# A four-layer graph network on one core: three engines and GpSimd put into the order of the source, and layer 0's products dealt out over the edge products

## The chip, the cores and the metric

The kernel runs on one core of a Trainium2 chip. The metric is device time in microseconds (us), the median of several runs. Engines are named as the profile names them: PE is TensorE's matmuls, PEld its weight loads, DVE is VectorE, ACT is ScalarE, POOL is GpSimd and SP is SyncE. In this kernel SP issues nearly all DMAs and computes nothing.

## The reference, cut to what matters

A graph of 3125 nodes with 128 features each and 103125 edges (src, dst, weight) goes through four layers. After each, the layer's output is added to its input and normalized over the features.

```python
# layer 0: weighted sum over the edges
out = relu(segment_sum(edge_weight[:, None] * (x @ weight)[src], dst) + b)
# layer 1: attention with 4 heads, softmax over the edges that reach a node
e = leaky_relu(a_s[src] + a_d[dst], 0.2); p = exp(e - segment_max(e)[dst])
out = segment_sum(h[src] * (p / segment_sum(p)[dst]), dst) + bias + x @ skip_W + skip_b   # then a layer norm of its own
# layer 2: dot-product attention over the edges
out = x + softmax_over_edges((x @ Wq)[dst] . (x @ Wk)[src] / sqrt(128)) applied to (x @ Wv), @ Wo
# layer 3: two mean aggregations, relu between them, sigmoid at the end
x = layernorm(x + layer(x))        # after every layer
```

## The kernel before, in words

**Dense matrices from the edges.** The nodes are padded to 25 blocks of 128. The kernel turns the edge list into two matrices in DRAM: `ctd`, how many edges join each source and each destination (bf16), and `wd`, the sum of their weights (f32), both with source rows and destination columns or the reverse as the layer needs them. After that every layer is made of dense products with these matrices.

**The edge stage.** The edges are sorted into 640 windows, which are worked off in 40 batches of 16 windows. A batch covers 80 rows of `wd`. For batch b, `make(b)` builds on DVE two one-hot tiles (`ohd`, `ohc`, line 824) and their products with three bf16 parts of the weight (`wod`, line 833); the last half of the third part is made by ACT (`more`, line 842). PE then multiplies, in four chunks of four windows, the counts (`cp`, 8 matmuls, line 864) and the weights (`wp`, 24 matmuls, line 872); `cp` and `wp` share three PSUM buffers. ACT copies them out to `cs` (line 877) and `ws` (line 883). In the source, one chunk stands as cp, wp, copy of cs, four ACT scalings for batch b+1, copy of ws. `make(b + 1)` is traced ahead of batch b's chunks. The one-hot tiles have two buffers, so DVE can be one batch ahead. At the end of a batch SP stores `ws` into `wd` (line 885, 1000 KB in two DMAs), and after every second one `cs` into `ctd` (line 888).

**Layer 0's products.** Beside this, layer 0 is begun: for each row block i of 128, `add0` loads its row of `wd` in two halves of ten column blocks (`cw`, line 790, three buffers of 640 KB) and adds 20 f32 products with `xw` to five PSUM banks (line 794). A block may be added at the end of batch b when (done+1)*128 <= (b-1)*80, that is when its last rows were made by batch b-2 at the latest. The remaining five column blocks (`left`) follow after the edge stage, in the first part of layer 1, with their own loads. Also in the edge stage stand `xw_of` (x times layer 0's weight, at the end of batches 0 and 1), `products_of_weights` and the bias products (batch 2) and `keys_of` (inside make(10), make(18), make(26)).

**The later layers.** Layer 1 goes over four groups of destination blocks, two head pairs each and 25 source blocks c; a step is one c. `masks` (ACT line 1225, DVE lines 1219 and 1226) runs two steps ahead of the products (lines 1236 and 1241). `values` (lines 1130 to 1144) prepares the operands of two source blocks: products on PE, two multiplications on DVE, and a split into three bf16 parts that goes back and forth between ACT and DVE (lines 549 to 555). In the first group it stands inside the steps. Smaller work (norms, transposes, skip products at line 1249) is hung into later steps with `later(k, f)`. Layer 2 has scores (line 1373), exp on ACT (line 1376), multiplication with the counts on DVE (line 1377) and f32 products (line 1381); layer 3 has two passes over `ctd` (lines 1476 and 1549).

**What sets the order.** Inside one tile context a scheduler orders every engine's instructions before the kernel is compiled: it takes the source's order as priority, but lets an instruction go ahead when an earlier one would still be waiting by its own estimate. It also puts in all semaphore waits. On the chip every engine then works off its list in that order.

Of the kernel before, what the change touches and what calls it, by code (L numbers as in the profile page):

```python
# [495 lines left out]
Z0 = 20  # L496
# [9 lines left out]
def fast_path(  # L506
# [4 lines left out]
    nc = tc.nc  # L511
# [46 lines left out]
    xw = cst.tile([P, NB, P], F32, name="f_xw")  # L558
# [184 lines left out]
    def xw_of(b0, n):  # L743

        t = zps.tile([P, 512], F32, name="trx", tag="acc0")
        for k in range(n):
            nc.tensor.transpose(t[:, k * P : (k + 1) * P], x[:, b0 + k, :], ident)
        xT = ep.tile([P, 512], F32, name="f_xTb", bufs=2)
        nc.scalar.copy(xT[:, : n * P], t[:, : n * P])
        t = zps.tile([P, 512], F32, name="trx", tag="acc2")  # L750
        for k in range(n):
            nc.tensor.matmul(t[:, k * P : (k + 1) * P], xT[:, k * P : (k + 1) * P], l0_wt, start=True, stop=True)
        nc.scalar.copy(xw[:, b0 : b0 + n, :].rearrange("p b d -> p (b d)"), t[:, : n * P])


    def layer_norm(lp, o, i, blocks, scalar=False):

        b0, n = blocks
        bs = lp.tile([P, n, 6], F32, name="bs")
        mv = lp.tile([P, n, 2], F32, name="mv")  # L760
        for b in range(n):
            nc.vector.bn_stats(bs[:, b, :], i[:, b0 + b, :])
        for b in range(n):
            nc.vector.bn_aggr(mv[:, b, :], bs[:, b, :])
        sd = lp.tile([P, n], F32, name="sd")
        nc.vector.tensor_scalar(sd, mv[:, :, 1], EPS, None, OP.add)
        nc.scalar.activation(sd, sd, AF.Sqrt)
        nc.vector.reciprocal(sd, sd)
        if scalar:
            ms = lp.tile([P, n], F32, name="ms")  # L770
            nc.vector.scalar_tensor_tensor(ms, mv[:, :, 0], -1.0, sd, OP.mult, OP.mult)
            for b in range(n):
                nc.scalar.activation(
                    o[:, b0 + b, :], i[:, b0 + b, :], AF.Identity, bias=ms[:, b : b + 1], scale=sd[:, b : b + 1]
                )
            return
        for b in range(n):
            nc.vector.tensor_scalar(o[:, b0 + b, :], i[:, b0 + b, :], mv[:, b, 0:1], sd[:, b : b + 1], OP.subtract, OP.mult)

    def bias0(acc, n):  # L780
        for j in range(n):
            nc.tensor.matmul(acc[:, j, :], ones, l0_br, start=(j == 0), stop=False, skip_group_check=True)

    def add0(pool, i, accs, blocks):

        b0, n = blocks
        for h in range(0, n, 10):
            m = min(10, n - h)
            cw = pool.tile([P, min(10, n), P], F32, name="cw")[:, 0:m]
            nc.sync.dma_start(  # L790
                cw.rearrange("p c d -> p (c d)"), wd[i * P : (i + 1) * P, (b0 + h) * P : (b0 + h + m) * P]
            )
            for j in range(h, h + m):
                nc.tensor.matmul(  # L794
                    accs[j // 4][:, j % 4, :], cw[:, j - h, :], xw[:, i, :], start=False,
                    stop=(i == NB - 1 and (j % 4 == 3 or j == n - 1)), skip_group_check=True,
                )

    def end0(acc, b0, n):
        t = lp0.tile([P, 4, P], F32, name="r0")  # L800
# [5 lines left out]
    zp = front.enter_context(tc.tile_pool(name="f_zp", bufs=3))  # L806
# [4 lines left out]
    def make(b):  # L811

        if b % 8 == 2 and 8 < b < NBT - 8:
            keys[b // 8 + 1] = keys_of(b // 8 + 1)
        kd2, kc2, w2, w3 = keys[b // 8]
        ohd = op_.tile([P, 2 * BW, P], BF16, name="ohd")
        ohc = op_.tile([P, 2 * BW, P], BF16, name="ohc")

        def twos(k):
            k = k[:, b % 8, :, :, :].rearrange("p q w t -> p (q w) t")  # L820
            return k[:, :, None, :].to_broadcast([P, 2 * BW, P // 2, 2])

        for o, k in ((ohd, kd2), (ohc, kc2)):
            nc.vector.tensor_tensor(
                o.rearrange("p w (a t) -> p w a t", t=2), twos(k),
                ramp.rearrange("p (a t) -> p a t", t=2)[:, None, :, :].to_broadcast([P, 2 * BW, P // 2, 2]),
                OP.is_equal,
            )
        wod = []
        for s in range(3):  # L830
            f = of_.tile([P, 2 * BW, P], BF16, name="wod")
            n = 2 * BW if s < 2 else BW
            nc.vector.tensor_tensor(  # L833
                f[:, 0:n].rearrange("p w (a t) -> p w a t", t=2), ohd[:, 0:n].rearrange("p w (a t) -> p w a t", t=2),
                twos(w2[s])[:, 0:n], OP.mult,
            )
            wod.append(f)

        def more(k):
            for w in range(k, k + 4):  # L840
                at = (b % 8) * BW + w
                nc.scalar.activation(wod[2][:, BW + w, :], ohd[:, BW + w, :], AF.Copy, scale=w3[:, 1, at : at + 1])  # L842

        return ohd, ohc, wod, more

    cs = None
    acc0 = None
    done = 0
    cur = make(0)
    for k in range(0, BW, 4):  # L850
        cur[3](k)
    for b in range(NBT):
        ohd, ohc, wod, _ = cur
        cur = make(b + 1) if b + 1 < NBT else None
        if b % SB == 0:
            cs = sp.tile([P, NB, SB * BW * WN], BF16, name="cs")
        ws = sp.tile([P, BW, P], F32, name="ws")
        for k in range(0, BW, 4):
            cp = cps.tile([P, 4, P], F32, name="cp", tag="cw")
            wp = cps.tile([P, 4, P], F32, name="wp", tag="cw")  # L860
            for j in range(4):
                for q in range(2):
                    w = q * BW + k + j
                    nc.tensor.matmul(  # L864
                        cp[:, j, 0:KW], ohd[:, w, :], ohc[:, w, 0:KW], start=(j == 0 and q == 0), stop=(j == 3 and q == 1),
                        skip_group_check=True,
                    )
            for j in range(4):
                for q in range(2):
                    w = q * BW + k + j  # L870
                    for s in range(3):
                        nc.tensor.matmul(  # L872
                            wp[:, j, :], ohc[:, w, :], wod[s][:, w, :], start=(j == 0 and q == 0 and s == 0),
                            stop=(j == 3 and q == 1 and s == 2), skip_group_check=True,
                        )
            i0 = (b % SB) * BW * WN + k * WN
            nc.scalar.copy(  # L877
                cs[:, :, i0 : i0 + 4 * WN].rearrange("p c (w i) -> p c w i", i=WN),
                cp[:, :, 0:KW].rearrange("p w (i c) -> p c w i", c=NB),
            )  # L880
            if cur:
                cur[3](k)
            nc.scalar.copy(ws[:, k : k + 4, :], wp)  # L883
        for a, e in ((0, 112), (112, KW)):
            nc.sync.dma_start(wv_[b * BW : (b + 1) * BW, a:e, :].rearrange("w k d -> k w d"), ws[a:e, :, :])
        if b % SB == SB - 1:
            i0 = (b - SB + 1) * BW * WN
            nc.sync.dma_start(ctd[:, :, i0 : i0 + SB * BW * WN].rearrange("c d i -> d c i"), cs)
        if b < 2:
            for blocks in GB[4 * b : 4 * b + 4]:  # L890
                xw_of(*blocks)
        if b == 2:
            products_of_weights()
            acc0 = [zps.tile([P, 4, P], F32, name=f"acc{k}", tag=f"acc{k}") for k in range(Z0 // 4)]
            for a in acc0:
                bias0(a, 4)
        while acc0 and (done + 1) * P <= (b - 1) * BW * WN:
            add0(zp, done, acc0, (0, Z0))
            done += 1
    for i in range(done, NB):  # L900
        add0(zp, i, acc0, (0, Z0))
    front.close()
# [147 lines left out]
    with ExitStack() as st:  # L1050
# [110 lines left out]
        for i in range(NB):  # L1161
            add0(tp, i, acc1, (Z0, NB - Z0))
            if i in marks:
                marks[i]()
            if i >= 13 and i % 3 == 1:
                values(ready)
                ready += 2
# [166 lines left out]
    with ExitStack() as st:  # L1334
# [79 lines left out]
        for x_, (q, c) in enumerate(items):  # L1414
# [6 lines left out]
            if q == 0 and NB - 4 <= c < NB - 1:  # L1421
                a = split + (c - NB + 4) * 512
# [157 lines left out]
@with_exitstack  # L1580
def gnn_kernel(ctx, tc, *args):

    nc = tc.nc
    fl = ctx.enter_context(tc.tile_pool(name="fl", bufs=1))
    flag = fl.tile([1, 1], I32, name="flag")
    fast_path(tc, flag, *args)
    ok = nc.values_load(flag[0:1, 0:1], min_val=0, max_val=1, skip_runtime_bounds_check_because="a comparison's result")
    with tc.If(ok == 0):
        general_path(tc, *args)
# [30 lines left out]
```

## Time and profile before

| | us |
|---|---|
| median of three runs | 1537.32 |
| lowest and highest | 1535.15 and 1537.59 |
| the profiled execution's own time | 1536.56 |
| its span in the profile | 1534.5 |
| PE busy (matmuls) | 1400.5 (91%) |
| PE weight loads busy | 1223.6 (80%) |
| DVE busy | 981.0 (64%) |
| ACT busy | 923.4 (60%) |
| POOL busy | 122.5 (8%) |

The span is what the profile covers; the execution's own time is 2.1 us longer. All positions below are us from the span's start. The edge batches run from about 43 to 469, layer 0's last products to 498, the first part of layer 1 to 548, layer 1's attention to about 968, layer 2 to 1257, layer 3 to the end. Two records stand for each f32 product on PE, since each is done in two passes in the trace, so 20 records of line 794 are ten products. A line such as `A <- B 21.1, 16, 1.7` in the list of waits says that A waited for B 21.1 us in all, 16 times, 1.7 us at the longest. A transfer's row in the time line gives the time in which SP was busy issuing it, not when it landed.

### The profile page before, as it was taken

The numbers are of one execution on the slowest core, as the hardware profiler recorded it, in microseconds if no ns is written. First come the engines' busy times: TensorE is split into PE (matmuls) and PEld (weight loads), VectorE is DVE, ScalarE is ACT, GpSimd is POOL, SyncE is SP. The second block draws the span as 40 slices with busy tenths as digits, with TensorE's granted clock in tenths as the row PEclk, the third lists the DMA queues.
The fourth block names the chain that finished last, engine by engine and source line by source line (L and its number), as shares of the span: only waits on it lengthen the run. The fifth ranks groups of instructions, "written<-read, shape, count | busy, mean of one in ns | idle before, by whom it ended". The sixth has DMA issues, their size and how long they took to land.

```text
span 1534.5 us, 35155 instructions
## 1 busy us (share of the span) xinstructions
PE 1400.5 (91%) x14871; PEld 1223.6 (80%) x14871; DVE 981.0 (64%) x1574; ACT 923.4 (60%) x1880; POOL 122.5 (8%) x136
## 2 busy tenths in 40 slices
PE   4899999999997978899989989899999989999995
PEld 3898999998997867899979889577777764458995
DVE  4999899989991389778878887544464360012005
ACT  2988778888882489878778676544474340023006
POOL 1000000000000023203311320300000000000000
PEclk9999999999999999999999999999999999999998
DMA  6387787878877623444434333332222226513551
GB/s 192 91 220 207 203 234 206 235 202 223 214 214 232 222 85 101 143 118 125 132 115 134 114 87 95 106 94 68 67 72 73 82 105 238 193 44 129 195 195 45
DMA packets 210368, 224.39 MB, mean 146 GB/s; under 512 B 72892, under 2 KB 184007, under 8 KB 209945
## 3 DMA queue, kind: packets, MB, share of 16 engines
q1 hardware_dynamic: 206344, 217.74, 48.4%
q10 hardware_dynamic: 3457, 2.35, 0.6%
q8 instruction: 118, 1.93, 0.5%
q0 software_dynamic: 400, 1.97, 0.4%
q14 instruction: 49, 0.40, 0.1%
HBM read 157.67 MB, written 64.36 MB: 145 GB/s over the span
## 4 chain that ended last, share of the span: by engine, by line
PE 40%; DVE 5%; ACT 2%; issue 1%; POOL 1%; DMA 1%; DVEq 0%; ACTq 0%; SPq 0%; POOLq 0%
PE acc L1381 9%; PE s L1373 8%; PE acc L1476 7%; PE acc L1549 6%; PE acc L1241 4%; PE acc L1236 2%; DVE cm L1226 1%; DVE nz L1260 1%; PE tr L1513 1%; PE acc L1513 1%; DMA ct<-f_ctd 1%; ACT fm L1225 1%; DVE cm L1219 0%; PE tr L1505 0%; PE acc L1505 0%
## 5 line engine op out<-in xcount | busy, mean ns | idle before, releaser
L1241 PE MATMUL acc<-vp,cm 128*128 128x198 bf16 x2500 | 344.7, 252 | 6.6 <-DVE cm L1226 4.1
L1225 ACT ACTIVATE fm<-adr,bas 128x896 bf16<-128x896 f32 (+1 forms) x320 | 286.5, 952 | 68.0 <-DVE cm L1226 63.1
L1236 PE MATMUL acc<-vp,ct 128*128 128x204 bf16 x1250 | 315.2, 256 | 10.0 <-DVE vp L1144 5.6
L1241 PEld LDWEIGHTS <-cm 128*128 128x128 bf16 x2500 | 236.0, 98 | 26.5 <-issue 10.6
L872 PE MATMUL wp<-wod,ohc 128*128 128x128 bf16 x3840 | 244.0, 219 | 8.8 <-ACT cs L877 6.6
L872 PEld LDWEIGHTS <-ohc 128*128 128x128 bf16 x3840 | 224.0, 98 | 9.8 <-issue 9.4
L833 DVE TENSOR_TENSOR wod<-ohd,w 128x4096 bf16<-128x4096 bf16 (+1 forms) x120 | 225.0, 1931 | 0.6 <-PE wp L872 0.6
L1226 DVE TENSOR_TENSOR cm<-fm,ct 128x896 bf16<-128x896 bf16 (+1 forms) x320 | 198.1, 649 | 36.1 <-PE acc L1241 14.1
L842 ACT ACTIVATE wod<-ohd,wu 128x128 bf16<-128x128 bf16 x640 | 197.0, 400 | 0.0
L1377 DVE TENSOR_TENSOR e<-e,ct 128x416 f32<-128x416 f32 (+1 forms) x175 | 110.4, 636 | 108.2 <-ACT e L1376 102.6
L1376 ACT ACTIVATE e<-s,f_nm 128x416 f32<-128x416 f32 (+1 forms) x175 | 111.5, 642 | 99.4 <-PE s L1373 94.1
L1381 PEld LDWEIGHTS acc<-self__8127,e 128*128 128x128 f32 x1250 | 148.4, 193 | 21.5 <-issue 19.7
L1373 PE MATMUL s<-yT,f_xT 128*128 128x416 f32 (+1 forms) x350 | 145.8, 552 | 4.6 <-ACT rt L1356 4.0
L1381 PE MATMUL acc<-self__8127,e 128*128 128x129 f32 x1250 | 148.7, 276 | 0.6 <-DVE e L1377 0.6
L794 PE MATMUL acc<-f_xw,cw 128*128 128x128 f32 x1000 | 118.4, 278 | 7.4 <-DMA cw<-wd 7.4
L1236 PEld LDWEIGHTS <-ct 128*128 128x128 bf16 x1250 | 122.4, 98 | 2.5 <-issue 1.5
L883 ACT COPY ws<-wp 128x512 f32<-128x512 f32 x160 | 93.6, 585 | 49.8 <-PE wp L872 48.2
L794 PEld LDWEIGHTS acc<-f_xw,cw 128*128 128x128 f32 x1000 | 115.0, 194 | 7.6 <-DMA cw<-wd 7.6
L864 PE MATMUL cp<-ohc,ohd 128*128 128x125 bf16 x1280 | 96.7, 218 | 21.1 <-ACT ws L883 17.9
L1373 PEld LDWEIGHTS s<-yT,f_xT 128*128 128x128 f32 x350 | 62.2, 191 | 57.7 <-issue 40.6
L1476 PE MATMUL acc<-ct,ip 128*128 128x512 bf16 (+1 forms) x525 | 104.9, 360 | 1.4 <-DMA ct<-f_ctd 1.4
L1549 PE MATMUL acc<-ip,ct 128*128 128x128 bf16 x1875 | 105.2, 219 | 0.0
(277 smaller groups left out, 1482.7 us busy)
## 6 DMA issues: line engine op xcount, KB each, us to landing
ct<-f_ctd SPq DMA_DIRECT2D x50, 800.0 KB
wd<-ws SPq DMA_DIRECT2D x40, 896.0 KB
ct<-f_ctd SPq DMA_DIRECT2D x150, 224.0 KB
cw<-wd SPq DMA_DIRECT2D x50, 640.0 KB
f_ctd<-cs SPq DMA_DIRECT2D x20, 1000.0 KB
ct<-f_ctd SPq DMA_DIRECT2D x25, 416.0 KB
ct<-f_ctd SPq DMA_DIRECT2D x25, 384.0 KB
cw<-wd SPq DMA_DIRECT2D x25, 320.0 KB
```

What stands on the lines that cost most here:

```text
L794: nc.tensor.matmul(accs[j // 4][:, j % 4, :], cw[:, j - h, :], xw[:, i, :], start=False, stop=(i == NB - 1 and (j % 4 == 3 or j == n - 1)) ...
L833: nc.vector.tensor_tensor(f[:, 0:n].rearrange("p w (a t) -> p w a t", t=2), ohd[:, 0:n].rearrange("p w (a t) -> p w a t", t=2), twos(w2[s] ...
L842: nc.scalar.activation(wod[2][:, BW + w, :], ohd[:, BW + w, :], AF.Copy, scale=w3[:, 1, at : at + 1])
L872: nc.tensor.matmul(wp[:, j, :], ohc[:, w, :], wod[s][:, w, :], start=(j == 0 and q == 0 and s == 0), stop=(j == 3 and q == 1 and s == 2), ...
L1225: nc.scalar.activation(f[:, : n * P], at, AF.Relu, bias=bas[:, c, h : h + 1], scale=UP)
L1226: nc.vector.tensor_tensor(m[:, : n * P], f[:, : n * P], ct[:, : n * P], OP.min)
L1236: nc.tensor.matmul(out_(F1, PW), ct[:, k * P : (k + 1) * P], vp[:, c, hp : hp + 2, :, 2 * F1 : V1], start=(c == 0), stop=False, skip_group ...
L1241: nc.tensor.matmul(out_(0, 2 * F1)[:, j], ms[j][:, k * P : (k + 1) * P], vp[:, c, hp + j, :, 0 : 2 * F1], start=False, stop=(c == NB - 1 a ...
L1373: nc.tensor.matmul(s[:, :m], xT[:, c * P : (c + 1) * P], yT[:, i0 * P + a : i0 * P + a + m], start=True, stop=True)
L1381: nc.tensor.matmul(acc[k // 3][:, (k % 3) * (P + 1) : (k % 3 + 1) * (P + 1)], es[q, c][:, k * P : (k + 1) * P], vo[:, c, 0 : P + 1], start ...
L1476: nc.tensor.matmul(acc[k][:, :n], ips[b // 4][:, b % 4, s, :], ct[:, c : c + n], start=(b == 0 and s == 0), stop=(b == NB - 1 and s == 2),)
L1549: nc.tensor.matmul(acc[g][:, j, :], ct[:, (b0 + j) * P : (b0 + j + 1) * P], ups[b // 4][:, b % 4, s, :], start=(b == 0 and s == 0 and j == ...
```

## The change

From a point just before the edge loop to the end of the fast path, PE, DVE, ACT and POOL take their instructions in the order of the source; SP is still ordered by the scheduler. `add0` is split: `adds0` issues the loads at once and returns a list of its products. In the edge loop these go to a list `todo`, from which four are issued after each chunk, so up to 16 in a batch. Blocks that are not due by the loop's end are added as before. The `left` products and all arithmetic stay as they were.

```diff
+    ctx.enter_context(
+        tc.manual_schedule(engines={mybir.EngineType.PE, mybir.EngineType.DVE, mybir.EngineType.Activation, mybir.EngineType.Pool})
+    )
     def layer_norm(lp, o, i, blocks, scalar=False):
...
-    def add0(pool, i, accs, blocks):
+    def adds0(pool, i, accs, blocks):
 
         b0, n = blocks
+        todo = []
         for h in range(0, n, 10):
             m = min(10, n - h)
             cw = pool.tile([P, min(10, n), P], F32, name="cw")[:, 0:m]
...
             for j in range(h, h + m):
-                nc.tensor.matmul(
-                    accs[j // 4][:, j % 4, :], cw[:, j - h, :], xw[:, i, :], start=False,
+                todo.append(lambda j=j, a=cw[:, j - h, :]: nc.tensor.matmul(
+                    accs[j // 4][:, j % 4, :], a, xw[:, i, :], start=False,
                     stop=(i == NB - 1 and (j % 4 == 3 or j == n - 1)), skip_group_check=True,
-                )
+                ))
+        return todo
+
+    def add0(*args):
+        for f in adds0(*args):
+            f()
...
     done = 0
+    todo = []
     cur = make(0)
...
             nc.scalar.copy(ws[:, k : k + 4, :], wp)
+            for f in todo[:4]:
+                f()
+            del todo[:4]
...
         while acc0 and (done + 1) * P <= (b - 1) * BW * WN:
-            add0(zp, done, acc0, (0, Z0))
+            todo += adds0(zp, done, acc0, (0, Z0))
             done += 1
+    for f in todo:
+        f()
     for i in range(done, NB):
         add0(zp, i, acc0, (0, Z0))
```

## The prediction

> **What bounds the kernel now.** I read the busy totals, then the stretches cut at the stage borders, then the waits inside the stretch that the change touches most, then SyncE's own time line, since SyncE alone stays free. The stretches (us, then busy us and instructions of PE, PEld, DVE, ACT, POOL, then clock, DMA share, GB/s):
>
> ```profile
> 43.00:83.00 40.00, 35.59 (x547) 33.95 (x547) 40.00 (x22) 37.22 (x108) 0.00 (x0) 1.00 0.50 129
> 83.00:469.00 386.00, 360.28 (x5466) 355.08 (x5465) 355.98 (x204) 319.63 (x879) 0.12 (x1) 1.00 0.81 217
> 469.00:498.00 29.00, 21.06 (x170) 20.60 (x170) 3.69 (x22) 2.21 (x4) 1.33 (x2) 0.88 0.74 218
> 498.00:548.00 50.00, 47.65 (x350) 41.30 (x351) 22.27 (x82) 22.76 (x50) 5.18 (x18) 0.93 0.61 193
> 548.00:600.00 52.00, 40.21 (x359) 34.12 (x357) 48.68 (x142) 49.34 (x91) 13.44 (x25) 0.93 0.30 90
> 600.00:968.00 368.00, 337.49 (x3564) 322.11 (x3563) 300.92 (x568) 278.64 (x368) 86.28 (x68) 0.98 0.40 117
> 968.00:1257.00 289.00, 282.98 (x1630) 209.98 (x1628) 137.78 (x319) 144.05 (x245) 8.63 (x5) 0.99 0.24 74
> ```
>
> The edge batches 4 to 39 (83 to 469) load PE to 93%, DVE to 92%, ACT to 83% and the DMA engines to 81%: four resources, none with much room. The first head pair of layer 1 (548 to 600) is DVE and ACT at 94%; what follows is PE's. So a stall on any one queue is paid. The waits of 83 to 469 (total, times, longest):
>
> ```profile
> DVE ohd L824 <- PE cp L864: 21.1, 16, 1.7
> PE cp L864 <- ACT ws L883: 17.9, 15, 1.6
> ```
>
> DVE waits for PE because layer 0's products run in lumps of 20 or 40 matmul records (two for each fp32 product), and PE waits for ACT after them. A lump, and SyncE around it:
>
> ```profile
> 148.19 2.09 SPq L885 DMA_DIRECT2D wd<-ws  x2
> ...
> 148.66 4.68 PE L794 MATMUL acc<-f_xw,cw 128*128 128x128 f32 x40
> ...
> 150.34 1.70 SPq L888 DMA_DIRECT2D f_ctd<-cs  x1
> 152.14 5.33 SPq L790 DMA_DIRECT2D cw<-wd  x2
> ```
>
> The cw load issued at 152.14 is used at 163.4, eleven us later and a whole batch after the place where the source has these products. The scheduler had moved PE's work to cover the load. At the edges' end it could not, and PE stood 7.37 us (PE's time line):
>
> ```profile
> 487.28 10.59 PE L794 MATMUL acc<-f_xw,cw 128*128 128x128 f32 x80 [7.37 <-DMA cw<-wd]
> ```
>
> **What the Trainium skill says.** "TensorE: Matmul & The Clock Gate", Architectural detail, has ACT and DVE as strict FIFOs and PE able to pull only weight loads ahead; here L794's weight loads start 0.06 us before their matmuls and nothing overtakes further. So a late operand holds all that is behind it. "Perfetto Trace Analysis", Identifying the Most-Contended Engine, prefers weight-load busy to matmul busy: 355.1 of 386 us, 92%, the same verdict. "DMA: Bandwidth & Descriptors", Anatomy of one DMA, gives 2.0 us plus bytes over 436 GB/s, an estimated 3.5 us for a 640 KB cw load; the trace is slower (below) and decides. "ScalarE: Activation LUTs", What ACT_TABLE_LOAD costs, has 2.7 us a load; here it is 1.283 us.
>
> **The change part by part.**
>
> *Spread products.* No instruction is added. The unit is 10 products in 2.29 us (20 records, start to next start), 0.229 each. One chunk of four windows is 8 cp and 24 wp matmuls, 1.78 us; a batch is 7.12. At 80 rows a batch and 128 a block come 12.5 products, 2.86 us: PE 9.98 us a batch. DVE has 9.93 (two ohd/ohc at 2.2, wod 5.53). Measured: 386/36 = 10.72. At best a batch falls to 10.0; with the three keys_of inside I take 10.2, 36 x 10.2 = 367, a gain of 19 before stalls.
>
> *The load's lead.* In the source, a block appended at the end of batch b meets PE after the first chunk of b+1, about 1.1 us after ws is copied (3.8 if four products are left over). The load: on an odd batch wd 2.09, ctd 1.70, first cw issue 4.85, then 4.0 from the end of the issue to the product (478.21 issue, 5.04 long, product at 487.28): 12.8 us after ws. On an even batch 7.7 (135.59 to 139.25, plus 4.0). Five blocks come in eight batches: two odd ones without leftover stall 11.7 each, one odd with leftover 9.0, the even 6.6 and 3.9: 42.9 us, 8.6 a block. For 21 blocks that is 180 us, the upper bound. The lower bound is nothing: the load needs only stores of batch b-2, SyncE is still free to be ordered, and it was seen to run ahead, the third adr load going out at 595.17, after 28 of the 50 ct loads that stand before it in the source. Against this, from block 2 on, each cw load in the trace stands directly behind the stores of its own batch, though SyncE had idle time earlier. But there PE's stand did not depend on it; with PE held, SyncE's queue runs empty and the loads become the only thing ready. I take 1.2 us a block, 25 us, and keep both ends.
>
> *In-order start.* xw_of (7 times) becomes a chain: transposes 0.45, ACT copy 0.6, matmuls 0.9, with the other copy between, 2.3 us, of which the trace has PE work for 1.4. Then products_of_weights, seven PE-ACT pairs, 5 us for 2.6 of work, bias 4.6. ACT's 2.12 us a chunk (cs 0.46, four wod 1.19, ws 0.47) sets batches without products, 8.5 us. From 45.3 (ohd of batch 1): 8.0 + 9.2 + 8.5 + 6.9 + 8.5 + 5 + 4.6 + 8.5, ends ACT's batch 3 at 104.5, and PE, a microsecond ahead of it, starts batch 4 near 103.5; it started at 82.9. Loss 20.6; DVE cannot run on, its ohd has two buffers.
>
> *Edge end.* Batch 39 ends at 103.5 + 367 + 25 = 496 (was 468.8). Block 23 then took 18.5 us; some 4 of them were SyncE held behind a cw buffer, now freed earlier: 14.5. Then 40 products, 9.2. Sum 520 against 498: **+22**.
>
> *498 to 548.* The scheduler filled the 6.0 us of the first left load (497.90 to 503.90) with scores1(0) and set left products into the 0.7 us copies between transposes and tr_sa. In source order 20 left products come first, scores1 waits for its copy five times (0.8 each), and both end0 chains (5.7 us, sqrt table 1.28 in it) precede the first mask. PE's fill of 6, five copies of 0.8 and a late mask of 2: **+12**, bounds +4 and +16.
>
> *values, 548 to 600.* One call is v 0.83, three ACT casts 0.63, two DVE subtractions 0.70, vp 0.64: a 4.95 us chain with DVE idle 2.0. Today cm work (0.4 each) stands in those holes. Nine calls, 18 us; the first holes are partly idle already: **+17**, bounds +8 and +22.
>
> *600 to 968.* PE's waits for the one bank "few" (L1249 9.9, L984 5.8 and 4.0) come from DVE and ACT running masks ahead; in source order these small steps precede the masks, a gain of up to 15. Against it each layer norm holds ACT: DVE statistics 2.2, then 7 Identity 2.8, against a lead of two steps, 3.7: about 2 us for each of six. **-5**, bounds -15 and +15. POOL's queue follows the same steps and has its cover: 86 busy of 368.
>
> *968 to 1257.* A part split in front of the exps (casts 0.63, subtractions 0.69) makes exps 3.3 us late; PE's fourth score waits for a PSUM buffer, 1.8 each, three times; norms with a table pair (2.6) cost more. **+10**, bounds 0 and +18. After 1257 the chain of waits already shows source order (L1505, L1506, L1513): 0.
>
> Sum +22 +12 +17 -5 +10 = +56 on the profiled execution's 1536.6 us (span 1534.5 and 2.1 around it), 1592.6; the median of the runs is 0.8 higher, so **1593**.
>
> **The rivals.** (1) *Loads keep their place behind the stores.* For it: every block from 2 on. Against: the adr load. It adds 155: 1748 in full; with half of the stalls shortened by idle DMA engines, about 1680. (2) *Faster: the lumps' waits vanish.* Place: batches 4 to 39; DVE never waits and runs at 9.93, 36 x 9.93 = 357.5 against 386, -28.5. It decides once loads are 8 us ahead, the start loses 10 rather than 21, and the rest sums to no more than +8 (each at its lower bound is -3): 1537 - 28.5 + 10 + 8 - 3 = 1523. For it: 21.1 and 17.9 us of waits. Against: the interleaving seen at values. (3) *The order was the source's already.* Then only the spread acts; layer 3 speaks for it, L1226 between L551 and L554 in layer 1 against it: within 3 us of 1537.
>
> **How the numbers follow.** Forecast 45% (its own range 1555 to 1635), rival 1 25%, rival 2 20%, rival 3 4%, and 6% for a loss under 18 us. 0.2% (3 us) is what a measurement of this kernel can tell from no change. Faster: rival 2 and a share of 3, 0.20; same 0.03; slower 0.77. The range goes from 1528, inside rival 2, to 1715, past the middle of rival 1: about a tenth is left out at either end.
>
> **What would show it.** Right: PE idle before L794 in short pieces released by cw, batch 4 near 103; L551, L554 and L1144 with no L1226 between them and DVE idle in 560 to 620; L1249's waits gone. Wrong: more than 5 us before each block (rival 1), or SyncE's cw loads ahead of the stores and batches of 10.0 us (rival 2). A first layer-1 product before 550 refutes the middle of the sum.

## The result, and the profile after

The changed kernel takes **1633.92 us** (median; 1632.13 to 1635.96) against 1536.99 for the kernel before on the same chip. The ratio is 1.0633, with a 95% interval of 1.0615 to 1.0652: 97 us slower. The span of the profiled execution went from 1534.5 to 1631.6 us, so the same 97 us can be looked for in the trace.

The stretches of the changed kernel, cut at its own stage borders (us; busy us and instructions of PE, PEld, DVE, ACT, POOL; clock, DMA share, GB/s). The first seven answer to the seven of before, in the same order; the last two are layer 3 from its first pass on.

```profile
41.00:107.00 66.00, 52.22 (x637) 48.95 (x638) 44.87 (x24) 41.98 (x116) 0.00 (x0) 0.92 0.31 83
107.00:486.00 379.00, 366.62 (x5515) 362.73 (x5513) 354.03 (x202) 320.41 (x879) 0.00 (x0) 1.00 0.85 224
486.00:510.00 24.00, 14.26 (x112) 14.06 (x109) 3.08 (x14) 2.80 (x5) 1.45 (x2) 0.79 0.68 195
510.00:567.00 57.00, 47.84 (x350) 41.43 (x348) 20.89 (x84) 21.25 (x46) 4.60 (x16) 0.94 0.52 167
567.00:658.00 91.00, 55.85 (x368) 45.30 (x369) 56.13 (x145) 53.73 (x93) 8.47 (x28) 0.76 0.18 54
658.00:1033.00 375.00, 338.44 (x3547) 322.45 (x3546) 310.50 (x564) 273.20 (x361) 78.53 (x61) 0.97 0.39 112
1033.00:1330.00 297.00, 289.04 (x1639) 212.59 (x1639) 143.07 (x310) 147.32 (x250) 14.45 (x11) 0.99 0.25 75
1330.00:1490.00 160.00, 149.96 (x800) 84.65 (x813) 32.66 (x89) 29.98 (x52) 0.00 (x0) 0.98 0.44 160
1490.00:1632.00 142.00, 104.65 (x1875) 104.47 (x1872) 22.23 (x104) 32.58 (x52) 0.00 (x0) 0.88 0.37 123
```

The edge batches (second line) became shorter: 379 us against 386. The fifth line is the worst: in the first group of layer 1 DVE and ACT were busy for nearly all of 53 us, and are now busy for 56 and 54 of 91. The work is nearly the same, but the two engines now do much less of it at the same time: counted from the records of both traces, they are busy together for 46.9 us of this stretch before and for 26.7 after. The clock there fell from 0.93 to 0.76, while PE's busy share fell from 77% to 61%.

Stage by stage, from the positions of the PE and DVE records (us). Runs of the experiments below stand in the same table. "Start" is the time of batch 4's first weight product. "Edge end" runs from the last weight product to the last product of layer 0's first 20 column blocks, and "to layer 1" from there to the first layer-1 product. A "group" of this table is one head pair of one group of destination blocks, so layer 1 has eight, 0 to 7, each ended by its `nz` (the DVE reductions that read its sums out of PSUM); "first group" is number 0. "Layer 2" runs from the last `nz` to layer 2's last product, and "middle" lies between layer 3's two passes. In the code cuts `g` counts the four groups of destination blocks instead.

| kernel | start | batches 4-39 | edge end | to layer 1 | first group | groups 1-7 | layer 2 | first pass | middle | second pass to end | median | ratio to before |
|---|---|---|---|---|---|---|---|---|---|---|---|---|
| before | 83.4 | 385.4 | 29.1 | 49.9 | 53.0 | 361.0 | 293.3 | 141.4 | 12.0 | 125.9 | 1536.99 | |
| changed | 107.0 | 379.3 | 23.7 | 57.3 | 90.3 | 375.5 | 296.9 | 141.8 | 18.0 | 141.8 | 1633.92 | 1.0633 |
| spread_only | 84.4 | 390.0 | 29.7 | 50.0 | 52.9 | 361.3 | 293.2 | 141.3 | 12.0 | 125.9 | 1541.22 | 1.0030 |
| edges_only | 107.5 | 381.0 | 24.8 | 48.5 | 52.8 | 360.0 | 293.4 | 141.4 | 12.0 | 126.3 | 1548.80 | 1.0074 |
| edges_lumps | 112.5 | 435.1 | 20.1 | 47.8 | 52.7 | 359.3 | 294.3 | 141.6 | 12.0 | 126.1 | 1602.48 | 1.0420 |
| edges_from3 | 82.2 | 393.3 | 24.6 | 48.3 | 53.0 | 359.0 | 294.2 | 141.7 | 12.0 | 126.1 | 1534.97 | 0.9983 |
| pace3 | 82.4 | 376.3 | 26.4 | 50.0 | 52.8 | 362.1 | 294.7 | 141.9 | 12.0 | 126.1 | 1522.08 | 0.9903 |
| pace3_lag | 81.8 | 372.5 | 28.9 | 48.4 | 52.9 | 360.7 | 294.7 | 141.9 | 12.0 | 126.4 | 1520.63 | 0.9891 |
| later_only | 83.4 | 385.4 | 30.0 | 57.2 | 90.5 | 375.5 | 297.0 | 141.9 | 18.0 | 141.7 | 1623.42 | 1.0565 |
| later_act_dve | 84.2 | 385.3 | 29.7 | 48.6 | 92.3 | 371.2 | 294.8 | 141.1 | 12.0 | 144.7 | 1607.53 | 1.0469 |
| later_pe | 83.9 | 385.3 | 29.9 | 54.1 | 54.4 | 366.4 | 297.7 | 141.7 | 16.3 | 123.1 | 1556.55 | 1.0144 |
| staged | 104.7 | 379.1 | 24.0 | 57.2 | 90.6 | 376.7 | 297.8 | 142.2 | 18.0 | 134.5 | 1629.58 | 1.0615 |
| staged2 | 107.3 | 379.4 | 23.9 | 57.2 | 67.2 | 386.7 | 297.6 | 142.2 | 18.0 | 134.5 | 1615.82 | 1.0511 |
| staged3 | 107.2 | 383.6 | 24.6 | 56.9 | 65.2 | 375.5 | 296.5 | 141.4 | 18.0 | 134.6 | 1604.68 | 1.0433 |

**The edges.** The waits of 107 to 486 in the changed kernel (total, times, longest):

```profile
ACT cs L888 <- PE cp L875: 32.1, 60, 3.6
ACT wod L852 <- DVE ohd L834: 18.1, 21, 1.4
DVE ohd L834 <- PE cp L875: 13.8, 3, 10.4
...
PE wp L883 <- DVE kc L534: 3.7, 3, 1.2
```

DVE's 16 waits behind the lumps are gone (three are left, one of them the late start). PE waits for cw, a load of layer 0, only once in those 379 us:

```profile
L799 PE MATMUL acc<-f_xw,cw 128*128 128x128 f32 x896 | 124.6, 282 | 2.8 <-DMA cw<-wd 2.8
```

The reason is SP's order (the time line of the changed kernel around one load):

```profile
265.71 0.34 SPq L795 DMA_DIRECT2D cw<-wd  x1
...
267.68 2.50 SPq L899 DMA_DIRECT2D wd<-ws  x2
...
277.98 6.29 SPq L899 DMA_DIRECT2D wd<-ws  x2
278.31 1.11 PE L799 MATMUL acc<-f_xw,cw 128*128 128x128 f32 x8
```

In the source this load stands behind the stores of batch 19, which begin at 277.98. It goes out 12.3 us ahead of them, even ahead of those of batch 18 (267.68), and 12.6 us before its first product. Of the 46 loads whose place is inside the edge loop, 38 go out ahead of the stores of their own batch; in the kernel before it was 3.

**The first group.** One turn of its pattern in the changed kernel, DVE and ACT only:

```profile
606.03 0.75 DVE L1150 TENSOR_TENSOR v<-trw,fa 128x256 f32<-128x256 f32 x2
...
606.86 0.63 ACT L549 CAST vp<-v 128x528 bf16<-128x528 f32 x1 [1.21 <-DVE v L1150]
...
607.53 0.71 DVE L551 TENSOR_TENSOR vs<-v,vp 128x528 f32<-128x528 f32 x1 [0.75 <-ACT vp L549]
...
608.27 0.63 ACT L552 CAST vp<-vs 128x528 bf16<-128x528 f32 x1 [0.77 <-DVE vs L551]
608.93 0.71 DVE L554 TENSOR_TENSOR vs<-vs,vp 128x528 f32<-128x528 f32 x1 [0.70 <-ACT vp L552]
609.68 0.63 ACT L555 CAST vp<-vs 128x528 bf16<-128x528 f32 x1 [0.78 <-DVE vs L554]
610.21 1.94 ACT L1241 ACTIVATE fm<-adr,bas 128x512 bf16<-128x512 f32 x3
610.34 0.45 DVE L1160 TENSOR_SCALAR vp<-vp 128x396 bf16<-128x396 bf16 x2 [0.70 <-ACT vp L555]
...
612.53 0.75 DVE L1150 TENSOR_TENSOR v<-trw,fa 128x256 f32<-128x256 f32 x2
```

Every bracket names the other engine: each of the two stands while the other works. Two steps take 6.5 us (606.03 to 612.53), later 7.2, with the masks of both steps after the chain.

### The profile page after: what moved, and what is told of

It is laid out like the page before. It is cut to its first block, busy times and chain, and to the rows that moved or that the text cites. A ratio compares the mean times of both kernels' runs of the same rounds, so it can differ in the third digit from the quotient of the medians.

```text
span 1631.6 us, 35071 instructions
## 1 busy us (share of the span) xinstructions
PE 1426.0 (87%) x14858; PEld 1242.4 (76%) x14871; DVE 1006.6 (62%) x1574; ACT 935.2 (57%) x1886; POOL 117.2 (7%) x136
## 4 chain that ended last, share of the span: by engine, by line
PE 41%; DVE 11%; ACT 9%; issue 2%; DMA 0%; ACTq 0%; DVEq 0%
PE s L1389 7%; PE acc L1397 7%; PE acc L1257 7%; PE acc L1492 6%; PE acc L1565 5%; PE acc L1252 4%; ACT fm L1241 3%; DVE cm L1242 3%; DVE nz L1276 1%; DVE cm L1235 1%; DVE e L1393 1%; ACT f_x L991 1%; DVE bs L977 1%; PE acc L1529 1%; ACT f_xw L991 1%
## 5 line engine op out<-in xcount | busy, mean ns | idle before, releaser
L1257 PE MATMUL acc<-vp,cm 128*128 128x198 bf16 x2500 | 363.4, 258 | 43.3 <-DVE cm L1242 28.8
L1252 PE MATMUL acc<-vp,ct 128*128 128x204 bf16 x1250 | 327.5, 262 | 8.4 <-DVE nz L1276 4.9
L1241 ACT ACTIVATE fm<-adr,bas 128x896 bf16<-128x896 f32 (+1 forms) x320 | 282.5, 951 | 30.0 <-DVE cm L1242 29.8
L1257 PEld LDWEIGHTS <-cm 128*128 128x128 bf16 x2500 | 243.5, 100 | 67.6 <-DVE cm L1242 35.8
L1242 DVE TENSOR_TENSOR cm<-fm,ct 128x896 bf16<-128x896 bf16 (+1 forms) x320 | 207.0, 674 | 60.5 <-ACT fm L1241 48.2
L852 ACT ACTIVATE wod<-ohd,wu 128x128 bf16<-128x128 bf16 x640 | 204.7, 396 | 22.5 <-DVE ohd L834 22.5
L799 PE MATMUL acc<-f_xw,cw 128*128 128x128 f32 x1000 | 138.7, 284 | 12.5 <-DMA cw<-wd 12.5
L799 PEld LDWEIGHTS acc<-f_xw,cw 128*128 128x128 f32 x1000 | 122.8, 195 | 12.9 <-DMA cw<-wd 12.9
L888 ACT CAST cs<-cp 128x500 bf16<-128x500 f32 x160 | 92.3, 577 | 39.2 <-PE cp L875 38.8
L834 DVE TENSOR_TENSOR ohd<-kd,ramp 128x4096 bf16<-128x4096 bf16 x40 | 91.4, 2284 | 24.5 <-PE cp L875 24.5
```

The lines of the kernel that those rows point to most:

```text
L799: todo.append(lambda j=j, a=cw[:, j - h, :]: nc.tensor.matmul(accs[j // 4][:, j % 4, :], a, xw[:, i, :], start=False, stop=(i == NB - 1 an ...
L1241: nc.scalar.activation(f[:, : n * P], at, AF.Relu, bias=bas[:, c, h : h + 1], scale=UP)
L1242: nc.vector.tensor_tensor(m[:, : n * P], f[:, : n * P], ct[:, : n * P], OP.min)
L1252: nc.tensor.matmul(out_(F1, PW), ct[:, k * P : (k + 1) * P], vp[:, c, hp : hp + 2, :, 2 * F1 : V1], start=(c == 0), stop=False, skip_group ...
L1257: nc.tensor.matmul(out_(0, 2 * F1)[:, j], ms[j][:, k * P : (k + 1) * P], vp[:, c, hp + j, :, 0 : 2 * F1], start=False, stop=(c == NB - 1 a ...
```

## The experiments

**Which part of the program.** The order was limited by closing its guard early or opening it late (the engines' names are shortened in these diffs).

```diff
 # spread_only: the guard is left out, the spread stays
-    ctx.enter_context(tc.manual_schedule(engines={PE, DVE, Activation, Pool}))
 # edges_only: the guard is closed after the edge loop
+    order.close()
     front.close()
 # later_only: the kernel before, with the guard opened here
+    ctx.enter_context(tc.manual_schedule(engines={PE, DVE, Activation, Pool}))
     front.close()
 # edges_from3: as edges_only, opened at batch 3
+        if b == 3:
+            order.enter_context(tc.manual_schedule(engines={PE, DVE, Activation, Pool}))
```

> The products are dealt out four to a chunk as in the changed kernel, but no engine is held to the source order. Theory A (the loss of 97 us of span comes from the source order, mostly where ACT and DVE hand short steps back and forth after the edges; the spread itself costs nothing): 1530 to 1540 us, the scheduler places the products by its own estimate anyway. Theory B (the spread products and their loads inside the edge batches carry the loss): over 1580. Theory C (the lumps' waits were worth something and the spread takes them away by itself): 1515 to 1528.

Measured: 1541.22 us, ratio 1.0030 (1.0018 to 1.0043). That is 4 us more than before and just outside theory A's range, all in the start and in the batches (390.0 against 385.4); what makes it slower was not followed up. Theories B and C fall. But the spread hardly reached the chip: from batch 8 on the batches of this trace hold 20 or no products, as in the kernel before, so the scheduler had gathered them into lumps again. An even spread without the source order was not run.

> The changed kernel with the source order ended after the edge loop; all later layers are ordered by the scheduler again. Theory A: last product of layer 0's first 20 column blocks near 510 as in the changed kernel, everything behind it as before, so 1537 + 12 = 1549 us (1543 to 1556). Theory B: near 1634. Theory D (the late start of the edges is all that the source order costs there and is hidden later): 1537.

Measured: 1548.80 us, ratio 1.0074 (1.0057 to 1.0090), last product of the first 20 column blocks at 513.3. The total is theory A's 1549, and the later stages are those of before to within 1.5 us; the last product came 3 us later than it had said.

> The edge loop is that of the kernel before (lumped products, the scheduler's order); the source order begins after it. Theory A: the loss behind the edges in full, 97.1 - 12.2 = 85 us of span, so 1622 us (1615 to 1628), with the values stretch (first layer-1 product to the last nz of the first group) near 90 us and the end of layer 3 some 16 us longer. Theory B: within 10 us of 1537. Theory C adds to A: with the edges as before it is 1622 as well.

Measured: 1623.42 us, ratio 1.0565 (1.0548 to 1.0583). The stages after the edges are those of the changed kernel to within 0.3 us: 90.5, 375.5, 18.0, 141.7 and the rest of the row. The two halves add up: 11.7 and 86.3 us over the median of before in these rounds (1537.13), 98.0 against 96.9 for the whole change. **Nearly nine tenths of the loss is made behind the edges.**

> The source order holds only from batch 3 to the end of the edge loop, with the spread products: batches 0 to 2, with the chains of xw_of and products_of_weights, are the scheduler's. Theory A: the 23.6 us of the late start are gone and the 11.4 us that batches 4 to 39 and the end of the edges gained stay: 1537 - 11 = 1526 us (1521 to 1533). If the gain of the batches was only the idle loads of a late start (theory D): 1537 to 1545.

Measured: 1534.97 us, ratio 0.9983 (0.9975 to 0.9992), no more than the 0.2% that can be told from no change. The start was regained in full (82.2), but 14 us of the batches went (393.3 against 379.3). The time lies between the ranges of theories A and D. Theory A's 1526 was wrong, since the gain of the batches did not stay, and theory D had the reason: the late start had helped the loads. In the changed kernel block 0's first load goes out at 80.5, ahead of the stores of batch 2 at 88.2, for products at 108.4. In edges_from3 it follows those stores and is used 7.7 us after its issue (77.0, 84.7). Block 2 is then caught in batch 7, which takes 18.55 us instead of 10.91, 7.6 of the 14 (PE's time line of edges_from3):

```profile
115.52 1.11 PE L796 MATMUL acc<-f_xw,cw 128*128 128x128 f32 x8
...
116.90 1.50 PE L883 MATMUL wp<-wod,ohc 128*128 128x128 bf16 x24
123.16 2.08 PE L796 MATMUL acc<-f_xw,cw 128*128 128x128 f32 x8 [4.75 <-DMA cw<-wd]
125.03 1.05 PE L875 MATMUL cp<-ohc,ohd 128*128 128x125 bf16 x8
125.87 2.77 PE L883 MATMUL wp<-wod,ohc 128*128 128x128 bf16 x24
...
130.00 1.50 PE L883 MATMUL wp<-wod,ohc 128*128 128x128 bf16 x24
```

Beside the 4.75 us of waiting, the same 8 products take 2.08 instead of 1.11 us and the 24 weight products 2.77 instead of 1.50: PE at about half speed for some 6 us. The Trainium skill, "TensorE: Matmul & The Clock Gate", Part 1: The HAM clock gate, says that an idle window of about 3.4 us halves PE's clock until a busy window has passed. This trace agrees: 123.0 to 129.5 has a granted clock of 0.55, and the stretch after it 1.00.

**What the spread is worth in source order.** The lumps were put back: the kernel before, with the order on the edge loop alone.

```diff
 # edges_lumps: the kernel before, and
+    order.enter_context(tc.manual_schedule(engines={PE, DVE, Activation, Pool}))
     cs = None
...
+    order.close()
     front.close()
```

> The kernel before with the source order over the edge loop alone: products in lumps of a block at the end of a batch, not dealt out, the later layers scheduled. Against edges_only (1548.8 us) it differs in the spread alone. Theory H (in source order it is the spread that gives the loads their lead; a lump meets PE just after its load is issued): a stall of 4 to 9 us for each of 21 blocks, with PE at half speed for some us after the longer ones, 1640 to 1740 us. Theory I (SyncE's loads run ahead whatever the place of the products, the spread only removes the lumps' waits of 21.1 us): 1550 to 1575.

Measured: 1602.48 us, ratio 1.0420 (1.0401 to 1.0439), between the ranges of the two theories: batches 4 to 39 take 435 us, 54 more than with the spread. These batches in edges_lumps (PE's waits for the loads, then the stretch) and in edges_only:

```profile
PE acc L794 <- DMA cw<-wd: 38.3, 10, 8.7
112.00:548.00 436.00, 382.18 (x5513) 373.35 (x5513) 350.55 (x202) 312.23 (x875) 0.34 (x2) 0.95 0.73 196
```

```profile
108.00:488.00 380.00, 367.52 (x5503) 363.58 (x5500) 353.49 (x202) 320.22 (x877) 0.00 (x0) 1.00 0.85 223
```

Not 21 long waits but four of 8.3 to 8.7 us and one of 2.3; the other five are under 0.6. The four are the only ones of the 46 loads that went out behind the stores of their own batch. The waits come to 38.3 us (2.8 in edges_only), and PE is busy for 14.7 us more with as many products, at a granted clock of 0.95 instead of 1.00: together nearly all of the 54. So the spread keeps the load's wait out of PE's queue once that queue may not be reordered. With the scheduler free, it did not reach the chip.

**How evenly.** One number was changed in edges_from3, then the start of the spread.

```diff
 # pace3
-            for f in todo[:4]:
-                f()
-            del todo[:4]
+            for f in todo[:3]:
+                f()
+            del todo[:3]
 # pace3_lag: pace3, and
+            if b > 4:
```

> Like edges_from3, but three products instead of four are issued after each chunk, so 12 in a batch where 12.5 come due. In edges_from3 the batches take 8.07, 9.01 or 10.91 us, as they hold 0, 8 or 16 products, and the first products of block 2 stand 4.8 us before their load and then run at half speed. Theory E (the spread is uneven, and the list runs empty so that each load is used as soon as it is issued): every batch near 10.1, wp end near 82 + 36 x 10.1 + 5 for keys_of = 451, leftover products fill the wait for the last loads, 24 us less than edges_from3, 1511 us (1504 to 1522). Theory F (DVE, whose work is 9.9 us a batch, and the loads set the batches): 1528 to 1536.

Measured: 1522.08 us, ratio 0.9903 (0.9887 to 0.9920). The batches became even: 22 of the 36 take 10.01 us, near the prediction's floor, where edges_from3 had 8.07, 9.01 and 10.91. Theory F falls. Of theory E the lead of the loads is what holds, not the evenness: a batch's time follows its products (8.07 us with 4, 9.01 with 8, 10.91 with 16, about 0.24 each), so uneven batches add up to no more than even ones. The 17 us that the batches gave against edges_from3 come from shorter waits for loads (batch 7 fell from 18.55 to 14.34 us, batch 33 from 16.90 to 10.01), from cheaper batches around keys_of, and from 23 products, some 5.5 us, that moved behind the loop, where the end of the edges grew by only 1.8. The run changed the pace and the lead together; they were not separated. The forecast of 1511 was 11 us short, mostly by two things: batch 7 still takes 14.3 us, with a wait of 2.48 for block 2 and a granted clock of 0.55 in the 3.6 us after it, and each of three keys_of costs 2.8 in its own batch and 1.1 in the two after it, where 5 had been set for all three.

> The kernel pace3, with the first product issued in batch 5 and not in batch 4, so that every load has a batch more of lead; 12 products more are left after the loop. In pace3 block 2 meets its load 2.5 us early in batch 7, PE then runs at half speed and batch 7 takes 14.3 us instead of 10.8, and PE waits 6.4 us for the last loads after the edges. If the lead was one batch too short: batch 7 at 10.8, 3.5 us off, and the 2.8 us of added leftover lie in the last wait: 1517 to 1519 us. If the three cw buffers hold the loads back instead, the stall moves: 1520 to 1524.

Measured: 1520.63 us, ratio 0.9891 (0.9875 to 0.9908). No cw wait is left before the loop's end; batches 4 to 39 give 3.8 us, of which the end of the edges takes 2.5 back: the added leftover did not fit into the last wait, and against pace3 the times can't be told apart. This version beats the kernel before by 1.1%: the source order holds only from batch 3 to the end of the edge loop, and the products are dealt out three to a chunk.

**Which queue, behind the edges.** As later_only, with fewer engines in the guard.

```diff
+    ctx.enter_context(tc.manual_schedule(engines={DVE, Activation}))   # later_act_dve
+    ctx.enter_context(tc.manual_schedule(engines={PE}))                # later_pe
```

> Edges as in the kernel before; behind them only ACT and DVE are held to the source order, PE and POOL are scheduled. Theory A (the loss behind the edges is made where ACT and DVE hand short steps back and forth in source order): most of the 86 us of later_only, 1600 to 1623, the values stretch near 88 us, the end of layer 3 near 140 us, and only the 6 us in the middle of layer 3 (PE filling the holes of the last products with the next pass) regained. Theory G (PE's order carries it): under 1570.

Measured: 1607.53 us, ratio 1.0469 (1.0451 to 1.0486). The order of these two alone brings 92.3 us in the first group, 371.2 in groups 1 to 7 and 144.7 at the end: 39, 10 and 19 us.

> Edges as in the kernel before; behind them only PE is held to the source order. Theory A: the middle of layer 3 is 6 us longer, the part before layer 1 some 5 us, the values stretch within 10 us of 53, the end of layer 3 as before: 1545 to 1562 us. Theory G: near 1615.

Measured: 1556.55 us, ratio 1.0144 (1.0121 to 1.0167). PE's order costs 4 us ahead of layer 1, 5 in groups 1 to 7, 4 in layer 2 and 4 in the middle of layer 3, and nothing at the end of it (3 us less than before). Theory A holds in both. The two runs lose 72.1 and 21.1 us against their own runs of before, 93 in sum against 86 for the whole order behind the edges, so the two orders are not quite independent. The order of GpSimd was not run by itself.

**Why the first group is long.** First the chain of the split was dealt out over three steps, and the tail of layer 3 paired (both cuts are shortened).

```diff
 # staged: values in the first group
-            split3(fp, lambda s: vp[:, b : b + n, :, s, 0 : 2 * F1], v, [P, n, H, 2 * F1], "vs", [P, 2, H, 2 * F1])
+            nc.scalar.copy(o(0), v)
+            later(1, lambda: part(1))      # one subtraction on DVE, one cast on ACT
+            later(2, lambda: part(2))
+            later(3, minus)
 # staged: end of layer 3
+            if g % 2 == 0 and g < len(GB) - 1:
+                continue
+            for b0, n in GB[g - g % 2 : g + 1]:
+                layer_norm(lp, x, r, (b0, n), True)
```

> The changed kernel with two chains taken apart in the source. First, in layer 1's first group the split of values is dealt out: one subtraction and one cast in each of the two next steps, the negation in the third, with masks between. Second, at the end of layer 3 two block groups share a pair of table loads: sigmoid of both, then the norms of both. Theory A: first layer-1 product to last nz of the first group 90 -> 60 to 70 us; second pass to the end 141.8 -> 126 to 130; together 35 to 45 us, 1634 -> 1590 to 1600. If the stretch is long for another reason (throttled PE clock, late first mask, scores of the last blocks): 80 to 88 us and 1610 to 1622.

Measured: 1629.58 us, ratio 1.0615 (1.0592 to 1.0637). The first group did not move at all (90.6). That was a miss: the length of the chain is not what costs. The waits of staged in 565 to 656 show what does:

```profile
DVE cm L1261 <- ACT fm L1260: 30.0, 39, 2.7
PE acc L1271 <- DVE vp L1169: 28.9, 9, 6.6
ACT vp L1164 <- DVE vs L1163: 26.4, 20, 2.1
```

ACT's cast waits for a DVE subtraction that stands behind two `cm` products; those wait for the `fm` that ACT has just issued. The engines take turns whatever the length of the chain. So the casts alone were moved behind the masks of their step:

```diff
 # staged2
-                nc.scalar.copy(o(s), t)
+                casts.append(lambda: nc.scalar.copy(o(s), t))
...
                 masks(*items[made])
+            while casts:
+                casts.pop(0)()
 # and: masks three steps ahead from the second group of destination blocks on
-            for y_ in range(x_ if x_ == 0 else x_ + 2, min(x_ + 3, len(items))):
+            while made < min(x_ + (4 if g else 3), len(items)):
```

> The kernel staged with two more edits. In layer 1's first group the DVE pieces of the split stand ahead of a step's masks, as in staged, but each cast of ACT now stands behind the step's masks; from the second group on the masks run three steps ahead of the products, not two. Theory J (lock-step: in staged ACT's cast waited 26.4 us for a DVE subtraction that stood behind two cm products, which waited 30.0 us for the fm just issued by ACT, so the two engines took turns; the length of the chain did not matter): two steps fall from 7.0 to about 5.6 us, first layer-1 product to last nz of the first group 90.6 -> 75 to 80, ACT's waits for the subtraction under 10 us. Theory K (the stretch is long for PE's throttled clock and the late first mask): 87 to 91. For groups 1 to 7, if the lead of two steps is too short for a norm's 4 to 5 us on ACT and DVE: 376.7 -> 362 to 370; if not, 374 to 379. Sum by theory J 1600 to 1610 us.

Measured: 1615.82 us, ratio 1.0511 (1.0494 to 1.0529). The first group fell to 67.2 us, 23 off, more than expected; two steps take 4.23 us (the pairs of `v` at 607.35 and 611.59 in its time line). The waits of staged2 in 560 to 660:

```profile
ACT vp L1167 <- DVE vs L1165: 7.0, 12, 0.8
DVE cm L1268 <- ACT fm L1267: 5.9, 10, 2.7
```

Theory J is shown: 26.4 and 30.0 us became 7.0 and 5.9 through the place of three casts, and the time in which DVE and ACT are busy together went from 23.3 us in staged to 45.1. Theory K falls for most of the stretch; what is left over the 53 us is in the main PE's wait for the first mask, 8.5 us in both (2.4 in the kernel before), and PE's waits for the negation, 15.0 (5.6 before). Whether the casts could have been moved without dealing the chain out was not run. The second edit did the reverse of what was expected: groups 1 to 7 went from 376.7 to 386.7 us. PE's waits for `nz` rose to 12.2 us there (4.0 in the changed kernel) and for a block's transposition after its norm to 10.7 (1.5): in source order a longer lead of the masks puts them in front of everything small.

> The kernel staged2 with the masks two steps ahead again throughout, and with the square root of each norm of groups 0 to 2 taken one step after its DVE statistics (its scaling one step later too). In the changed kernel ACT stands 31.0 us in six pieces in groups 1 to 7 for the DVE step just before that root (5.2 each), with the next masks' fm queued behind it. Theory L (this hand-over costs the 14.5 us of groups 1 to 7): 375.5 -> 360 to 367. Theory M (it is covered by PE's work; the loss comes from other waits, such as the one PSUM bank of the turns): 372 to 377. The first group as in staged2, 67 us. Sum 1592 to 1599 by L, 1603 to 1608 by M.

```diff
 # staged3: staged2 with the masks two steps ahead again, and in norm1 of the first three groups of destination blocks
-        nc.scalar.activation(sd, sd, AF.Sqrt)
+            later(1, root)
```

Measured: 1604.68 us, ratio 1.0433 (1.0416 to 1.0451), which is the removal of the three-step lead and no more. Groups 1 to 7 took 375.5 us as in the changed kernel, although ACT's wait ahead of the root fell from 31.0 to 20.6. Theory L's numbers did not come, and theory M's did; but a third of the wait is all that the edit took away.

**Groups 1 to 7, as far as they are known.** The waits of ACT and PE in this stretch, of the kernel before (601 to 962):

```profile
ACT fm L1225 <- DVE cm L1226: 63.1, 61, 5.0
...
PE few L1249 <- DVE f_xw L1250: 9.9, 6, 3.4
...
PE acc L1241 <- DVE cm L1226: 2.6, 5, 0.8
```

and of the changed kernel (658 to 1033):

```profile
ACT fm L1241 <- DVE cm L1242: 29.8, 34, 2.4
...
PE acc L1257 <- DVE cm L1242: 14.7, 8, 3.9
...
PE few L1265 <- DVE f_xw L1266: 2.8, 5, 1.0
```

Before, ACT ran so far ahead that it stood for 63 us until buffers came free, and PE hardly ever waited for a mask; now ACT has half of that in hand and PE waits 14.7 us. This is not the whole loss: from the stretches (331.07 us of PE's work in the 361 before, 338.44 in the 375 after), PE stands 6.6 us longer in all, and is busy 7.4 us longer with nearly the same number of products, at a granted clock of 0.97 instead of 0.98. Which of the small steps eats the lead was not found: a third off the wait for the root of the norms brought nothing, a lead of three steps makes it worse, and later_pe shows that 5 of the 14.5 us come from PE's own order.

**The end of layer 3.** ACT's table loads in the second pass, before and changed:

```profile
L1568 ACT ACT_TABLE_LOAD x4 | 5.1, 1283 | 0.1
L767 ACT ACT_TABLE_LOAD x4 | 5.1, 1283 | 0.7 <-DVE sd L766 0.5
```

```profile
L771 ACT ACT_TABLE_LOAD x7 | 9.0, 1283 | 9.9 <-DVE sd L770 9.9
L1584 ACT ACT_TABLE_LOAD x6 | 7.7, 1283 | 0.1
```

In source order each block group goes through sigmoid and norm by itself, one after the other, and each brings its own two tables. The scheduler had put two groups into each pair. With the pairing written into the source (staged), 4 and 3 loads are left and the tail falls from 141.8 to 134.5 us: 7.3 us for the six saved loads (6 x 1.283 = 7.7), where 12 to 16 had been expected. The other 8.6 us of the loss were not separated; ACT's wait for DVE ahead of the root's table, 9.9 us against 0.7 before, is still 5.3 in staged.

## Why the prediction was right, and where its steps were off

The sign, the range and the refusal of both large rivals held. The measured time is 41 us above the forecast, at the upper edge of the likeliest case's own range, and the loss lies elsewhere than forecast: 22 of the 56 us were set for the edges, which cost 12 of 97. By its steps:

- **In-order start, +20.6: measured +23.6** (batch 4 at 107.0). The step held, and edges_from3 regains it (82.2).
- **Batches 4 to 39, 367 + 25 of waits for loads: measured 379.3.** Both terms were off, and by luck in opposite directions. The waits were 2.8 us. The 367 was some 9 too low: PE's work at about 0.24 us a product sums to 363, as against 359; each of the three keys_of cost 4.0 us with the batch after it (12.68 and 11.22 us for 9.01 and 10.91), 12 in all where some 7 had been left; and three batches took 0.7 more. pace3 gives the floor of 10.0 a batch that it named, with 12 products.
- **Edge end: +22 in sum, measured +12.2** for the last product (510.1 against 497.9), by the batches; the end itself took the 23.7 us that the sum gave it.
- **498 to 548, +12: measured +7.4**; PE's order alone brings 4.2 of it (54.1 in later_pe), that of ACT and DVE alone nothing (48.6). The late mask that the step held at 2 us makes PE wait 8.46 us (2.4 before), and this falls into the next stretch.
- **values, +17: measured +37.3.** This is the term that was mis-sized. Some 6 of the 37 are the late first mask. Its DVE holes were right: 7.3, 6.8 and 6.8 us, 2.1 for each chain (whose 4.95 us are 4.76 by the parts that it lists). It left out that ACT stands too (13.6, 7.5 and 7.5 us) and that the masks can't run in either hole, so the chain and the masks of two steps come one after the other. staged and staged2 show that the cause is the turn-taking and not the length of the chain.
- **Groups 1 to 7, -5: measured +14.5.** The gain was there in part (L1249's 9.9 us became 2.8), but the loss, priced at 2 us for each of six norms, is larger: PE's waits for masks rose by 12, its idle time in all by 6.6, and its busy time by 7.4. Shortening the wait for the norms' root (staged3) brought nothing; what makes the loss stays open.
- **Layer 2, +10: measured +3.6.**
- **Layer 3, 0: measured +22.3** (0.4 in the first pass, 6.0, 15.9). The step that failed is "the chain of waits already shows source order". A chain shows only its own instructions. In the middle of layer 3 the scheduler had put the next pass's first products into the holes of the last ones, and at the end it had paired the block groups; neither lay on the lines of the chain that were read.

**Rival 1** (loads behind the stores) fails by the 2.8 us of waits. Its mechanism is real, though: edges_lumps pays more than 8 us for each of four loads behind their stores, and edges_from3 4.75 us and more for one. **Rival 2** saw the loads rightly: they ran ahead of the stores, which the prediction had named as a sign against itself, and the lumps' waits went. But its own term gave 6 us of the 28.5, since the batches took 10.54 us each and not 9.93, and the rest of its sum failed as well. (That sum counts the rest twice, as +8 and as -3; with +8 alone it is 1526.5.) **Rival 3** is refuted by the first group alone.

## What to carry to other kernels

Holding an engine to the source order is a choice for a stretch, not for a program: here it helps where one engine is nearly full and the other queues feed it (the edge batches, once the products stand far enough behind their loads), and it costs where two engines hand short steps to each other in both directions. In such a loop, try each engine's dependent step behind that engine's independent work of the same turn; cutting the chain into pieces without doing so changed nothing here. A chain of waits doesn't show whether two queues were reordered: compare each engine's sequence with the source.

## What the runs showed of the hardware

PE's wait of 4.75 us in edges_from3 was paid for again: some 6 us at half speed, 2.9 us more (0.97 on the 8 products, 0.45 on 8 cp, 1.27 on 24 wp, 0.19 on the next products). A wait of 2.48 us in pace3 was followed by about half speed as well (a granted clock of 0.55 over 3.6 us), so a wait shorter than the page's window can be enough. In the stretch of the changed kernel where PE is busy for 61% of the time its granted clock is 0.76; before, it was 0.93 at 77%. A table load of ACT takes 1.283 us in both kernels, and six fewer of them shortened a tail in which ACT and DVE take turns by 7.3 us.
